# Layer 1's norm of the next image, cut into steps between the attention units

## The chip, the cores and the metric

One core of a Trainium2 chip runs the whole network on a batch of 8 images. The metric is the device time of one execution in microseconds (us), as the median of several runs.

## The reference, cut to what matters

Four residual layers work on x of shape (8, 56, 56, 192). The change concerns layer 1 alone: a group norm over groups of six channels (`_gn`), then a layer norm over the channels inside `_L1_conv_ref`, then shifted-window attention with 7 x 7 windows, 6 heads of 32 channels.

```python
x = x + _L1_conv_ref(_gn(x), ...)      # layer 1

mu = jnp.mean(x, axis=-1, keepdims=True)
var = jnp.var(x, axis=-1, keepdims=True)
x = (x - mu) * jax.lax.rsqrt(var + EPS) * gamma + beta
sx = jnp.roll(x, shift=(-SHIFT[0], -SHIFT[1]), axis=(1, 2))
# windows of 7 x 7, q, k, v by one projection, softmax(q k^T + bias + mask) v, projection, roll back
```

## The kernel before, in words

The layers run one after the other, each image by image, all in float32. Layer 1 lies between about 3000 and 4750 us of the profile.

An image of layer 1 is a tile `x1` of 128 partitions: two half images of 64 channels by three channel chunks j. `rolled` (L489) loads it from DRAM with the shift applied, in 18 DMAs whose rows hold 53 or 3 floats; the same function stores the result in another 18. All 36 are issued on SP's queue. The pool gives `x1` two buffers, so the load of image b+1 needs the buffer of image b-1, which comes free when the store of image b-1 has landed.

`layer1_norm` (L499) makes the normed image `xr`:

- statistics: 12 `bn_stats` on VectorE (L170), aggregates (L171), 14 small matmuls `gh_m` and 14 `gh_v` that sum over channel groups (L181), a square root on ScalarE (L192);
- for each g of four groups of 392 positions: three ScalarE operations that scale and reorder into windows (L516), matmuls for the mean (L523, tile `mean`), a subtraction on VectorE (L525), a square on ScalarE (L527), matmuls for the variance (L529, tile `vps`);
- one square root over all groups (L533), one reciprocal (L534), and for each g a matmul that spreads the result (L538, tile `rstd`) and a multiplication (L540).

The attention of an image is four units, g = 0 to 3, one for each row of windows in both halves. `layer1_scores(g)` (L543) projects q and k (L556), v (L576), forms the scores `S` (L596) and their softmax on VectorE, POOL and ScalarE (L603 to L611). `layer1_mix(g)` (L614) transposes the weights (L626, tile `et_ps`), multiplies with v (L639, `po`), projects (L658, `pr`) and adds into `x1` (L663). The scores of a unit are issued ahead of the mix of the unit before it: scores(u+1), mix(u). The norm of image b+1 is issued as a whole at g = 1 of image b, ahead of scores(b,2) and mix(b,1); the store of image b follows mix(b,3).

The order on each engine is made by the tile framework at build time. It works through the program with costs of its own and lets an instruction pass an earlier one that isn't ready. PSUM tiles come from two tags. Tag "mm" has three buffers: `gh_m`, `gh_v`, `mean`, `rstd`, `qk_ps`, `v_ps`, `po` and `pr` take turns in it. Tag "et" has two: `et_ps`, and before the change `vps`. On the chip every engine, and SP's queue, then works strictly in the order that was made.

Of the kernel before, what the change touches and what calls it, by code (L numbers as in the profile page):

```python
# [10 lines left out]
F32 = mybir.dt.float32  # L11
AF = mybir.ActivationFunctionType
# [8 lines left out]
TT = 392  # L21
# [55 lines left out]
def kernel(ctx: ExitStack, tc: tile.TileContext, a: dict, out: bass.AP):  # L77
    nc = tc.nc
    nimg = a["x"].shape[0]
# [28 lines left out]
    eps5 = const.tile([128, 1], F32, name="eps5")  # L108
# [22 lines left out]
    x2 = [dram.tile([C, NT], F32, name=f"x2_{b}") for b in range(nimg)]  # L131
# [30 lines left out]
    def gn_stats_halves(x, pool, psum, sc, sh, ptag="qv"):  # L162

        n = x.shape[2]
        nt = -(-n // 512)
        st = pool.tile([128, 3, nt, 6], F32, name="gh_st")
        mv = pool.tile([128, 3, 2], F32, name="gh_mv")
        for j in range(3):
            for t in range(nt):
                nc.vector.bn_stats(st[:, j, t, :], x[:, j, bass.ts(t, n // nt)])  # L170
            nc.vector.bn_aggr(mv[:, j, :], st[:, j].rearrange("p t s -> p (t s)"))  # L171

        def over_groups(v, name):
            if ptag == "mm":
                ps = psum.tile([128, 512], F32, name=name, tag="mm", bufs=3)[:, 0:3]
            else:
                ps = psum.tile([128, 2, 512], F32, name=name, tag=ptag)[:, 0, 0:3]
            for j in range(3):
                ks = [k for k in range(3) if abs(j - k) < 2]
                for k in ks:  # L180
                    nc.tensor.matmul(ps[:, j:j + 1], gmath[:, k, j, :], v[:, k:k + 1], start=(k == ks[0]), stop=(k == ks[-1]))  # L181
            return ps


        mean = pool.tile([128, 3], F32, name="gh_mean")
        nc.vector.tensor_scalar(mean, over_groups(mv[:, :, 0], "gh_m"), n / NH, None, ALU.mult)
        d = pool.tile([128, 3], F32, name="gh_d")
        nc.vector.tensor_tensor(d, mv[:, :, 0], mean, ALU.subtract)
        nc.vector.tensor_tensor(d, d, d, ALU.mult)
        nc.vector.tensor_tensor(d, d, mv[:, :, 1], ALU.add)  # L190
        if n == NH:
            nc.scalar.activation(sc, over_groups(d, "gh_v"), AF.Sqrt, bias=eps5)  # L192
        else:

            z = pool.tile([128, 3], F32, name="gh_z")
            nc.vector.scalar_tensor_tensor(z, mean, 1.0 - n / NH, mean, ALU.mult, ALU.mult)
            nc.vector.scalar_tensor_tensor(z, over_groups(d, "gh_v"), n / NH, z, ALU.mult, ALU.add)
            nc.scalar.activation(sc, z, AF.Sqrt, bias=eps5)
        nc.vector.reciprocal(sc, sc)
        nc.vector.scalar_tensor_tensor(sh, mean, -1.0, sc, ALU.mult, ALU.mult)  # L200
# [288 lines left out]
    def rolled(dram_image, tile_image, store):  # L489

        d = dram_image.rearrange("(j p) (h w) -> p j h w", p=64, w=W)
        for s, h0, h1, r0 in ((0, 0, 28, 3), (1, 0, 25, 31), (1, 25, 28, 0)):
            for w0, w1, c0 in ((0, 53, 3), (53, 56, 0)):
                for j in range(3):
                    sb = tile_image[64 * s:64 * s + 64, j, h0:h1, w0:w1]
                    dr = d[:, j, r0:r0 + h1 - h0, c0:c0 + w1 - w0]
                    nc.sync.dma_start(dr, sb) if store else nc.sync.dma_start(sb, dr)  # L497

    def layer1_norm(b, pool, psum, consts):  # L499

        ones2, ones32, sel = consts[4:]
        x = pool.tile([128, 3, H // 2, W], F32, name="x1")
        rolled(x1[b], x, False)
        sc = pool.tile([128, 3], F32, name="sc1")
        sh = pool.tile([128, 3], F32, name="sh1")
        gn_stats_halves(x.rearrange("p j h w -> p j (h w)"), pool, psum, sc, sh, "mm")

        xr = pool.tile([128, 3 * NH + 16], F32, name="xr")
        nc.gpsimd.memset(xr[:, 3 * NH:], 0.0)
        xw = xr[:, 0:3 * NH].rearrange("p (j n) -> p j n", j=3)  # L510

        vps = psum.tile([128, 512], F32, name="vps", tag="et", bufs=2)
        for g in range(4):
            gs = bass.ts(g, TT)
            for j in range(3):
                nc.scalar.activation(  # L516
                    xw[:, j, gs].rearrange("p (w i j) -> p w i j", i=7, j=7),
                    x[:, j, 7 * g:7 * g + 7].rearrange("p i (w j) -> p w i j", j=7), AF.Identity,
                    bias=sh[:, j:j + 1], scale=sc[:, j:j + 1],
                )  # L520
            mp = psum.tile([128, 512], F32, name="mean", tag="mm", bufs=3)[:, 0:TT]
            for j in range(3):
                nc.tensor.matmul(mp, ones2, xw[:, j, gs], start=(j == 0), stop=(j == 2))  # L523
            xs = xw[:, :, gs]
            nc.vector.tensor_tensor(xs, xs, mp.unsqueeze(1).to_broadcast([128, 3, TT]), ALU.subtract)  # L525
            sq = pool.tile([128, 3, TT], F32, name="sq")
            nc.scalar.activation(sq, xs, AF.Square)  # L527
            for j in range(3):
                nc.tensor.matmul(  # L529
                    vps[32 * g:32 * g + 32, 0:TT], ones32, sq[:, j], start=(j == 0), stop=(j == 2)  # L530
                )
        rs = pool.tile([128, TT], F32, name="rs1")
        nc.scalar.activation(rs, vps[:, 0:TT], AF.Sqrt, bias=eps5)  # L533
        nc.vector.reciprocal(rs, rs)  # L534
        for g in range(4):
            gs = bass.ts(g, TT)
            bp = psum.tile([128, 512], F32, name="rstd", tag="mm", bufs=3)[:, 0:TT]
            nc.tensor.matmul(bp, sel[32 * g:32 * g + 32], rs[32 * g:32 * g + 32], start=True, stop=True)  # L538
            xs = xw[:, :, gs]
            nc.vector.tensor_tensor(xs, xs, bp.unsqueeze(1).to_broadcast([128, 3, TT]), ALU.mult)  # L540
        return x, xr

    def layer1_scores(g, xr, pool, psum, S, es, consts):  # L543

# [409 lines left out]
    with ExitStack() as st:  # L954
        pool = st.enter_context(tc.tile_pool(name="qv", bufs=2))
        psum = st.enter_context(tc.tile_pool(name="qvp", bufs=4, space=PSUM))
# [4 lines left out]
        x = layer0_load(0, pool)  # L961
# [7 lines left out]
        for b in range(nimg):  # L969

            between = {i: blocks.pop(0) for i in (1, 7, 12) if blocks}
            ahead = []
            if b + 1 < nimg:
                x = layer0_load(b + 1, pool)
# [5 lines left out]
    with ExitStack() as st:  # L980
        pool = st.enter_context(tc.tile_pool(name="mix", bufs=2))
        psum = st.enter_context(tc.tile_pool(name="mixp", bufs=2, space=PSUM))
# [10 lines left out]
    with ExitStack() as st:  # L993
        pool = st.enter_context(tc.tile_pool(name="l1", bufs=2))
        psum = st.enter_context(tc.tile_pool(name="l1p", bufs=1, space=PSUM))
        consts = layer1_weights(pool, psum)

        ones2 = pool.tile([128, 128], F32, name="ones2", bufs=1)
        ones32 = pool.tile([128, 32], F32, name="ones32", bufs=1)
        sel = pool.tile([128, 128], F32, name="sel", bufs=1)  # L1000
        nc.gpsimd.memset(ones2, 0.0)
        nc.gpsimd.memset(ones32, 0.0)
        for s in range(2):
            nc.gpsimd.memset(ones2[64 * s:64 * s + 64, 64 * s:64 * s + 64], 1.0 / C)
            nc.gpsimd.memset(ones32[64 * s:64 * s + 64, 16 * s:16 * s + 16], 1.0 / C)
        nc.gpsimd.dma_start(sel, a["sel"])
        S = psum.tile([128, 24, 64], F32, name="S")
        nc.vector.memset(S, 0.0)
        es = [[pool.tile([128, 24, 64], F32, name=f"e{k}{s}", bufs=1) for s in range(2)] for k in range(2)]
        for e in es[0] + es[1]:  # L1010
            nc.gpsimd.memset(e, 0.0)

        consts = (*consts, ones2, ones32, sel)
        normed = {0: layer1_norm(0, pool, psum, consts)}
        units = [(b, g) for b in range(nimg) for g in range(4)]
        values = {units[0]: layer1_scores(0, normed[0][1], pool, psum, S, es, consts)}
        for u, (b, g) in enumerate(units):
            if g == 1 and b + 1 < nimg:
                normed[b + 1] = layer1_norm(b + 1, pool, psum, consts)
            if u + 1 < len(units):  # L1020
                b1, g1 = units[u + 1]
                values[b1, g1] = layer1_scores(g1, normed[b1][1], pool, psum, S, es, consts)
            layer1_mix(g, normed[b][0], values.pop((b, g)), pool, psum, es, consts)
            if g == 3:
                rolled(x2[b], normed.pop(b)[0], True)


    with ExitStack() as st:
        pool = st.enter_context(tc.tile_pool(name="l2i", bufs=2))
# [135 lines left out]
```

## Time and profile before

| | us |
|---|---|
| median of 3 runs (lowest, highest) | 8218.3 (8207.87, 8222.58) |
| the profiled execution, its own time | 8152.04 |
| its span | 8149.2 |
| TensorE (PE) busy in the span | 6370.0 (78%) |
| VectorE (DVE), ScalarE (ACT), POOL busy | 3182.6, 1734.7, 480.4 |

The timeline gives the moments of each middle image b: when SP issues the first store of image b-1, the first `bn_stats` for image b+1, the first L516 of its norm, the first q/k matmul of unit (b,2), which stands behind that norm, and the next image's first store.

| image b | first store | first L170 | first L516 | qk of (b,2) | next first store |
|---|---|---|---|---|---|
| 1 | 3281.7 | 3339.5 | 3352.2 | 3395.5 | 3499.8 |
| 2 | 3499.8 | 3559.3 | 3571.9 | 3614.7 | 3722.2 |
| 3 | 3722.2 | 3781.7 | 3794.3 | 3836.7 | 3944.7 |
| 4 | 3944.7 | 4003.2 | 4015.8 | 4057.7 | 4163.4 |
| 5 | 4163.4 | 4222.6 | 4235.5 | 4278.3 | 4384.6 |
| 6 | 4384.6 | 4443.8 | 4456.6 | 4499.2 | 4607.4 |

Read along a row: the image's period is last column less first. Image 0 needs no wait, as both buffers of `x1` are free then; its norm of image 1 runs from 3125.0 (end of the last L663 of unit (0,0)) to 3172.3 (qk of unit (0,2)).

### The profile page before, as it was taken

How to read it: one execution, taken by the hardware profiler on the slowest of the kernel's cores; microseconds unless marked ns; L12 is line 12 of the kernel's file. 1: busy time of each engine (PE TensorE's matmuls, PEld its weight loads, DVE VectorE, ACT ScalarE, POOL GpSimd, SP SyncE). 2: the span in 40 equal slices, each digit the busy share in tenths (PEclk: the TensorE clock that was granted, in tenths of full speed). 3: DMA queues.
4: the chain of work that ended last, by engine and by line, in shares of the span. 5: the costliest groups of instructions: out<-in, count | busy, mean ns of one | idle time of the engine just before them, and what ended most of it. 6: DMA issues, size and time to landing. Idle time of an engine off the chain costs nothing.

```text
span 8149.2 us, 126312 instructions
## 1 busy us (share of the span) xinstructions
PE 6370.0 (78%) x56258; PEld 4179.1 (51%) x56258; DVE 3182.6 (39%) x4598; ACT 1734.7 (21%) x2448; POOL 480.4 (6%) x390
## 2 busy tenths in 40 slices
PE   6799787787877868777777858799968646678899
PEld 4567555555655544444444534566634336644444
DVE  6677522221212224333333346555557540033321
ACT  2234211111111112222222200111135310023333
POOL 4200000000000001111111200000000000000000
PEclk8899888888888878777777878899988758889999
DMA  8998967666677540333333255554458667732221
GB/s 200 196 190 165 191 138 160 148 138 139 133 150 168 121 83 25 49 43 49 43 49 49 44 102 183 183 178 169 168 136 190 150 190 169 173 109 72 71 57 27
DMA packets 1042080, 1018.65 MB, mean 125 GB/s; under 512 B 833812, under 2 KB 964796, under 8 KB 1015272
## 3 DMA queue, kind: packets, MB, share of 16 engines
q1 hardware_dynamic: 1018016, 829.64, 44.4%
q10 hardware_dynamic: 11808, 118.60, 6.8%
q0 software_dynamic: 11712, 62.34, 3.0%
q8 instruction: 441, 7.23, 0.4%
q14 instruction: 103, 0.84, 0.0%
HBM read 668.34 MB, written 342.04 MB: 124 GB/s over the span
## 4 chain that ended last, share of the span: by engine, by line
PE 55%; DMA 17%; DVE 12%; SPq 6%; issue 5%; ACT 4%; POOL 2%; DVEq 0%; POOLq 0%; ACTq 0%
PE op L401 6%; PE qv L349 5%; DMA rt<-toep 5%; PE y L438 5%; PE po L938 5%; PE ph L929 4%; PE cps L872 4%; PE pj L418 4%; SPq L497 4%; PE qk_ps L556 3%; PE mx L755 3%; PE cv L735 3%; DVE ln_st L206 2%; PE pr L658 2%; DMA rt<-qvw 2%
## 5 line engine op out<-in xcount | busy, mean ns | idle before, releaser
L401 PE MATMUL op<-rt,lt 120*56 120x56 f32 x9216 | 683.6, 313 | 319.2 <-DMA rt<-toep 217.3
L401 PEld LDWEIGHTS op<-rt,lt 120*56 120x56 f32 x9216 | 659.6, 224 | 403.7 <-issue 386.4
L349 PE MATMUL qv<-w_qv_sb,xn 64*112 64x288 f32 x5376 | 729.0, 425 | 107.2 <-DVE act L355 107.2
L349 PEld LDWEIGHTS qv<-w_qv_sb,xn 64*112 64x112 f32 x5376 | 556.5, 183 | 277.0 <-DVE act L355 133.2
L418 PE MATMUL pj<-xn,w_p_sb 64*128 64x392 f32 (+1 forms) x1920 | 491.0, 540 | 85.8 <-ACT pp L423 46.7
L872 PE MATMUL cps<-zc,wt 113*128 113x224 f32 x1536 | 322.7, 374 | 210.4 <-DMA zc<-ones_d 165.2
L407 DVE COPY o<-op 120x448 f32<-120x448 f32 (+1 forms) x160 | 99.6, 622 | 902.1 <-PE op L401 886.6
L938 PE MATMUL po<-hid,w_sb 128*64 128x392 f32 x2304 | 398.6, 505 | 52.6 <-ACT hid L933 52.6
L929 PE MATMUL ph<-y,w_sb 64*128 64x392 f32 x2304 | 422.2, 499 | 6.5 <-ACT hid L933 6.5
L438 PE MATMUL y<-pp,w_o_sb 128*64 128x392 f32 (+1 forms) x1920 | 420.7, 517 | 3.6 <-DVE pp L432 1.6
L872 PEld LDWEIGHTS cps<-zc,wt 113*128 113x128 f32 x1536 | 307.7, 201 | 225.4 <-issue 214.2
L356 ACT ACTIVATE act<-act 112x576 f32<-112x576 f32 x448 | 301.1, 683 | 509.5 <-DVE act L355 508.9
L355 DVE TENSOR_TENSOR act<-qv,b_qv 112x576 f32<-112x576 f32 x448 | 317.2, 749 | 39.9 <-PE qv L349 39.9
L556 PE MATMUL qk_ps<-xr,wg 64*96 64x392 f32 x1536 | 327.7, 529 | 3.3 <-ACT qk L562 2.3
L418 PEld LDWEIGHTS pj<-xn,w_p_sb 64*128 64x128 f32 (+1 forms) x1920 | 203.4, 185 | 245.4 <-issue 115.7
L735 PE MATMUL cv<-zc,wt 128*128 128x224 f32 x1536 | 301.2, 355 | 29.9 <-DMA zc<-pd 29.9
L929 PEld LDWEIGHTS ph<-y,w_sb 64*128 64x128 f32 x2304 | 232.4, 189 | 171.5 <-issue 25.9
L423 ACT ACTIVATE pp<-pj,vecs_sb 128x784 f32<-128x784 f32 (+1 forms) x160 | 146.8, 918 | 787.7 <-PE pj L418 754.5
L735 PEld LDWEIGHTS cv<-zc,wt 128*128 128x128 f32 x1536 | 290.2, 189 | 46.3 <-issue 39.3
L938 PEld LDWEIGHTS po<-hid,w_sb 128*64 128x64 f32 x2304 | 164.9, 140 | 282.4 <-issue 223.8
L945 DVE TENSOR_TENSOR x<-x,z 128x392 f32<-128x392 f32 x96 | 54.4, 567 | 643.4 <-ACT z L943 643.4
L693 PE MATMUL pin<-w_in_sb,xn 64*128 64x384 f32 x1392 | 257.1, 516 | 57.3 <-POOL xn L684 38.2
(218 smaller groups left out, 8675.2 us busy)
## 6 DMA issues: line engine op xcount, KB each, us to landing
lt<-toep SPq DMA_DIRECT2D x72, 896.0 KB
rt<-toep SPq DMA_DIRECT2D x72, 896.0 KB
qvh<-qv SPq DMA_DIRECT2D x224, 252.0 KB
qvw<-qv SPq DMA_DIRECT2D x448, 126.0 KB
lt<-qvh ACTq DMA_DIRECT2D x72, 784.0 KB
rt<-qvw ACTq DMA_DIRECT2D x72, 784.0 KB
wt<-in_band_dram SPq DMA_DIRECT2D x24, 2048.0 KB
pd<-pt SPq DMA_DIRECT2D x8, 5568.0 KB
```

Source lines behind the costliest of these rows:

```text
L349: nc.tensor.matmul(ps[s][:, which, 0:D1 // 2], xn[64 * s:64 * s + 64, j, bass.ts(i, 2 * W)], w_qv[64 * s:64 * s + 64, j, which, ns], start ...
L355: nc.vector.tensor_tensor(act, ps[s][:, :, 0:D1 // 2], b_qv[:, :, ns], ALU.add)
L356: nc.scalar.activation(act, act, AF.Silu)
L401: nc.tensor.matmul(op[64 * u:64 * u + W, i, :], lt[0:120, :, d], rt[0:120, :, d], start=True, stop=True)
L418: nc.tensor.matmul(ps[0:M, s, 0:TT], w_p[64 * s:64 * s + 64, j, d0:d0 + M], xn[64 * s:64 * s + 64, j, ts], start=(j == 0), stop=(j == 2),)
L438: nc.tensor.matmul(y[64 * s:64 * s + 64], w_o[0:M, c, 64 * j:64 * j + 64], pp[0:M, s], start=(c == gated[0][0]), stop=(c == gated[-1][0]),)
L497: nc.sync.dma_start(dr, sb) if store else nc.sync.dma_start(sb, dr)
L556: nc.tensor.matmul(ps[s], wg[64 * s:64 * s + 64, j, c0:c0 + HC], xw[64 * s:64 * s + 64, j, gs], start=(j == 0), stop=(j == 2),)
L735: nc.tensor.matmul(dst, wt[:, c4 + i, 128 * q:128 * q + 128], zc[:, :, c4 + i, q:q + NPAIR], start=(q == 0), stop=(q == 1),)
L872: nc.tensor.matmul(dst.rearrange("p (b n) -> p b n", n=NPAIR), wt[:, c4 + i, (3 - q) * OP:(4 - q) * OP], zc[:, :, c4 + i, q:q + NPAIR], st ...
L929: nc.tensor.matmul(ps[:, s, 0:TT], w0[64 * s:64 * s + 64, j, m * 128:(m + 1) * 128], y[64 * s:64 * s + 64, j, ts], start=(j == 0), stop=(j ...
L938: nc.tensor.matmul(ps[64 * s:64 * s + 64], w1[:, m, 64 * j:64 * j + 64], hid[:, m, s], start=(m == 0), stop=(m == 5),)
```

## The change

`layer1_norm` becomes a generator that stops (`yield`) after the issue of the load, after the statistics, after each group's square, after each group's square root, after the reciprocal, and after each group's last multiplication. The driving loop takes these steps by a plan of three numbers for each unit: `first` and `second` steps ahead of the scores, `third` steps between scores and mix. The driver's order for a middle image b is, after the store of image b-1:

- g = 0: load(b+1), statistics(b+1), scores(b,1), both parts of group 0, mix(b,0)
- g = 1: both parts of group 1, scores(b,2), both parts of group 2, mix(b,1)
- g = 2: both parts of group 3, reciprocal, scores(b,3), last step of group 0, mix(b,2)
- g = 3: last step of group 1, scores(b+1,0), last steps of groups 2 and 3, mix(b,3), store(b)

The variance tile moves from tag "et" to tag "mm", one for each group in place of one for all, and the square root is taken group by group on 32 partitions. The memset of the padding of `xr` and the tile of `rs` are made ahead of the statistics.

```diff
     def layer1_norm(b, pool, psum, consts):
...
         rolled(x1[b], x, False)
+
+        xr = pool.tile([128, 3 * NH + 16], F32, name="xr")
+        nc.gpsimd.memset(xr[:, 3 * NH:], 0.0)
+        xw = xr[:, 0:3 * NH].rearrange("p (j n) -> p j n", j=3)
+        rs = pool.tile([128, TT], F32, name="rs1")
+        yield x, xr
...
         gn_stats_halves(x.rearrange("p j h w -> p j (h w)"), pool, psum, sc, sh, "mm")
-
-        xr = pool.tile([128, 3 * NH + 16], F32, name="xr")
-        nc.gpsimd.memset(xr[:, 3 * NH:], 0.0)
-        xw = xr[:, 0:3 * NH].rearrange("p (j n) -> p j n", j=3)
-
-        vps = psum.tile([128, 512], F32, name="vps", tag="et", bufs=2)
+        yield
         for g in range(4):
...
             nc.scalar.activation(sq, xs, AF.Square)
+            yield
+            vp = psum.tile([128, 512], F32, name="vps", tag="mm", bufs=3)[32 * g:32 * g + 32, 0:TT]
             for j in range(3):
-                nc.tensor.matmul(
-                    vps[32 * g:32 * g + 32, 0:TT], ones32, sq[:, j], start=(j == 0), stop=(j == 2)
-                )
-        rs = pool.tile([128, TT], F32, name="rs1")
-        nc.scalar.activation(rs, vps[:, 0:TT], AF.Sqrt, bias=eps5)
+                nc.tensor.matmul(vp, ones32, sq[:, j], start=(j == 0), stop=(j == 2))
+            nc.scalar.activation(rs[32 * g:32 * g + 32], vp, AF.Sqrt, bias=eps5[32 * g:32 * g + 32])
+            yield
         nc.vector.reciprocal(rs, rs)
+        yield
         for g in range(4):
...
             nc.vector.tensor_tensor(xs, xs, bp.unsqueeze(1).to_broadcast([128, 3, TT]), ALU.mult)
-        return x, xr
+            yield
...
-        for u, (b, g) in enumerate(units):
-            if g == 1 and b + 1 < nimg:
-                normed[b + 1] = layer1_norm(b + 1, pool, psum, consts)
-            if u + 1 < len(units):
-                b1, g1 = units[u + 1]
-                values[b1, g1] = layer1_scores(g1, normed[b1][1], pool, psum, S, es, consts)
-            layer1_mix(g, normed[b][0], values.pop((b, g)), pool, psum, es, consts)
-            if g == 3:
-                rolled(x2[b], normed.pop(b)[0], True)
+        plan = [(1, 1, 2), (1, 1, 2), (1, 2, 1), (0, 1, 2)]
+        for b in range(nimg):
+            x = images[b][0]
+            steps = layer1_norm(b + 1, pool, psum, consts) if b + 1 < nimg else iter(())
+            for g in range(4):
+                first, second, third = plan[g]
+                for _ in range(first):
+                    ahead = next(steps, None)
+                    if ahead:
+                        images.append(ahead)
+                for _ in range(second):
+                    next(steps, None)
+                following = None
+                if g < 3 or b + 1 < nimg:
+                    xr = images[b][1] if g < 3 else images[b + 1][1]
+                    following = layer1_scores((g + 1) % 4, xr, pool, psum, S, es, consts)
+                for _ in range(third):
+                    next(steps, None)
+                layer1_mix(g, x, values, pool, psum, es, consts)
+                values = following
+            for _ in steps:
+                pass
+            rolled(x2[b], x, True)
```

More of the change, by code (lines that the diff above doesn't have):

```diff
@@ L1013 @@
         consts = (*consts, ones2, ones32, sel)
-        normed = {0: layer1_norm(0, pool, psum, consts)}
-        units = [(b, g) for b in range(nimg) for g in range(4)]
-        values = {units[0]: layer1_scores(0, normed[0][1], pool, psum, S, es, consts)}
-        for u, (b, g) in enumerate(units):
-            if g == 1 and b + 1 < nimg:
-                normed[b + 1] = layer1_norm(b + 1, pool, psum, consts)
-            if u + 1 < len(units):
-                b1, g1 = units[u + 1]
-                values[b1, g1] = layer1_scores(g1, normed[b1][1], pool, psum, S, es, consts)
-            layer1_mix(g, normed[b][0], values.pop((b, g)), pool, psum, es, consts)
-            if g == 3:
-                rolled(x2[b], normed.pop(b)[0], True)
+        steps = layer1_norm(0, pool, psum, consts)
+        images = [next(steps)]
+        for _ in steps:
+            pass
+        values = layer1_scores(0, images[0][1], pool, psum, S, es, consts)
+        plan = [(1, 1, 2), (1, 1, 2), (1, 2, 1), (0, 1, 2)]
[18 more added lines that the diff above has]
+                values = following
+            for _ in steps:
+                pass
+            rolled(x2[b], x, True)
     with ExitStack() as st:
```

## The prediction

> **What bounds the kernel now.** I read the page first (TensorE is busy 78% of the span and leads the chain of work that ended last), then the windows of one image of layer 1, then the timeline of that image, then TensorE's waits. The windows of image 2, cut at the store's start, the norm's first L516, the first qk behind the norm and the next store (columns: window, its length, busy time and count of PE, PEld, DVE, ACT, POOL, then clock, DMA share, GB/s):
>
> ```profile
> 3499.80:3571.90 72.10, 44.48 (x705) 28.39 (x701) 23.29 (x42) 10.66 (x17) 8.71 (x4) 0.68 0.88 85
> 3571.90:3614.70 42.80, 28.82 (x81) 11.43 (x81) 12.59 (x11) 15.73 (x21) 0.00 (x0) 0.78 0.00 1
> 3614.70:3722.20 107.50, 93.77 (x1988) 58.46 (x1989) 43.70 (x55) 28.92 (x46) 26.21 (x13) 0.82 0.11 36
> ```
>
> In the last window, three attention units, PE is busy 93.77 of 107.5 us: the units are bound by PE, with some 4.6 us idle each. The first two windows hold one unit and the norm, and there PE waits. In the timeline (start, length, engine, line, what, in brackets the idle time before it and its releaser):
>
> ```profile
> 3499.80 34.87 SPq L497 DMA_DIRECT2D x<-x  x18
> ...
> 3536.01 26.23 SPq L497 DMA_DIRECT2D x<-x  x18
> ...
> 3546.80 0.63 DVE L663 SCALAR_TENSOR_TENSOR x<-pr,bpr,x 128x392 f32<-128x392 f32 x1 [1.35 <-PE pr L658]
> 3559.28 4.34 DVE L170 BATCH_NORM_STATS2 gh_st<-x 128x6 f32<-128x392 f32 x9 [11.86 <-DMA x<-x]
> ...
> 3563.93 3.22 PE L181 MATMUL gh_m<-gh_mv,gmath_sb 128*128 128x1 f32 x14 [17.17 <-DVE gh_mv L171]
> ...
> 3568.08 3.12 PE L181 MATMUL gh_v<-gh_d,gmath_sb 128*128 128x1 f32 x14 [0.94 <-DVE gh_d L190]
> ...
> 3572.73 4.20 PE L523 MATMUL mean<-xr,ones 128*128 128x392 f32 x6 [1.54 <-ACT xr L516]
> ...
> 3579.62 3.67 PE L529 MATMUL vps<-sq,ones 128*32 128x392 f32 x6 [2.69 <-ACT sq L527]
> ...
> 3590.89 2.14 PE L523 MATMUL mean<-xr,ones 128*128 128x392 f32 x6
> ...
> 3609.91 1.68 PE L538 MATMUL rstd<-rs,sel 32*128 32x392 f32 x6 [3.31 <-DVE rs L534]
> ...
> 3614.65 3.69 PE L556 MATMUL qk_ps<-xr,wg 64*96 64x392 f32 x8
> ```
>
> Two things are to be seen. First, x of image b+1 can't arrive before some 60 us after the end of image b-1: 18 stores (34.87 us) and, on the same queue and into the buffer that they free, 18 loads (26.23 us). Unit (b,0) covers 47 us of that; then everything waits. Second, no qk matmul passes the norm. Its inputs were there long before, and PE stood idle for 17.17, 2.69 and 3.31 us while `gh_m`, `vps` and `rstd` weren't ready, with all three "mm" buffers free at the first and the third. Only the transposes L626, whose tag is "et", slip in, and even they come after the first `vps`, which stands ahead of them in that tag. In all of layer 1 the first matmuls into the tiles of one tag stand in the order of the code. I take it as the rule of this plan: **buffers of one tag are handed out in program order, so an "mm" tile whose data is late holds back every later "mm" tile.**
>
> TensorE's waits from 3395 to 4607 us, which hold five norms (waiter, releaser, total, times, longest):
>
> ```profile
> PE gh_m L181 <- DVE gh_mv L171: 101.9, 5, 22.8
> PE po L639 <- issue: 40.3, 20, 3.7
> PE vps L529 <- ACT sq L527: 27.2, 10, 2.8
> PE rstd L538 <- DVE rs L534: 16.6, 5, 3.3
> ```
>
> **What the Trainium skill says.** "DMA: Bandwidth & Descriptors", Specifications: full rate needs at least 512 bytes in a piece. The rows here are 212 and 12 bytes, and while they move the DMA engines are taken 0.88 of the time at 85 GB/s: agrees. "TensorE: Matmul & The Clock Gate", What's actually happening: after an idle window PE runs at half rate until it has been busy for some 3.4 us. The first six `mean` matmuls after the wait take 4.20 us, later ones 2.14: agrees. "ScalarE: Activation LUTs", Table sets: exp followed by sqrt needs a table load each way. The trace has 16 loads in layer 1, two for each image, at 1.283 us.
>
> **The change part by part**, for a middle image, counted from the first store (S).
>
> 1. *Load and statistics ahead of scores(b,1).* SP's order stays: the load stood right behind the store already, so nothing is gained there; the bias loads that follow it aren't needed until S(b,1). POOL's memset of 0.11 us waits for nothing late. But `gh_m` and `gh_v` are now ahead of `qk_ps` of scores(b,1) in "mm". PE waits for x; queued behind the wait are all of scores(b,1) and the `po` and `pr` of mix(b,0), and through them DVE's, ACT's and POOL's work on them. Before, that unit ran during store and load. From 3499.80 to the end of `gh_v` (3571.2) it is **71.4 us**; the other images agree within 1.5.
> 2. *Cold clock* for the first qk: `mean` showed 2.1 us lost. **+2.5**, between 0 and 4.
> 3. *Unit (b,0)* now runs behind the wait, free of the store's traffic. Plain units (qk to qk: 3428.7 to 3501.7, 3649.6 to 3725.1, 3871.6 to 3947.3, two each) take 36.5, 37.75 and 37.85: **37.4**. The 48 transposes of mix(b,0), tag "et", can run during the wait: 24 of them were 4.3 us of PE's time in the old norm; **-5**, between 0 and -7.
> 4. *The other three units*: qk of (b,2) to the next store is 104.3, 107.5, 108.0, 105.7, 106.3, 108.2 in the six images, mean **106.7**; the 24 transposes of mix(b,1) no longer ride in a norm: **+2**.
> 5. *The norm's matmuls between the units*, N. Warm, four `mean` groups at 2.14, four `vps` at 2.16 and `rstd` at 1.7 make 18.9 us of PE. Part lands where PE idles: the wait ahead of `po` is up to 3.7 us, and `mean`/`vps` of groups 0 and 2 stand just ahead of `po`: -6, between 0 and -10. But in groups 1 and 3 `vps` follows `mean` with only transposes between, as qk is behind both: the subtraction (1.38) and the square (1.18) are open, 2.8 us as in the trace, twice: +5.6, between 0 and +10. Four square roots on ACT in place of one (0.587 each; on 32 partitions I take the same) and the table goes back and forth up to eight more times (1.283 each) ahead of copies that free "mm" buffers: some 12 us of ACT, which has 72% free; +3 on PE, between 0 and +6. VectorE's work is unchanged and hidden by PE. **N = 21.5**, between 9 and 35.
>
> Sum: 71.4 + 2.5 + 37.4 - 5 + 106.7 + 2 + 21.5 = 236.5 us. Before, the six periods from 3281.7 to 4607.4 average 220.95. **+15.5 us for each of six images, +93.** What was saved (47 - 21.5 of the norm's own time) is less than the cover that unit (b,0) gave.
>
> 6. *Image 0* has its second x early (landed by about 3040), so no wait: its norm took 47.3 us alone; now 6 for the statistics' matmuls, 2 for transposes and N: **-17.8**. Norm 0 and image 7 are as before.
>
> Total +75 us. Against the profiled execution's own 8152.04 that is 8227; the median of runs, 8218.3, lies 66 us above that execution, and I add the same 75 to it: **8293 us**.
>
> **The rivals.**
> - *A: the order isn't binding* (other side: faster). If scores(b,1) pass the waiting `gh_m`, x lands behind their cover and nothing waits: four units of 37.4, 4 for the first unit under the store's traffic (41.6 on average), 2, N and 6 for `gh`: 183 us, -38 for each of six images and -18: 7973. It decides if the first qk of (b,1) starts before x has landed, S+60. For it: PE's idle time is that large. Against: the tag order, kept without exception through long idle times.
> - *B: a wash.* The wait is as forecast, but the norm's matmuls nearly all fall into idle PE time: N about 10 to 14 puts the total (7N - 75) within 16 us: 8218. For it: 4.6 idle us in each unit. Against: half of that is short drains ahead of transposes and `pr`, where no norm matmul stands.
> - *C: the steps hurt the units*, through table loads and `vps` waits, N = 35: +170, 8388. For it: ScalarE's copies free the buffers of every qk and v. Against: ACT is busy 29 of 107 us.
>
> **How the numbers follow.** Forecast with C as its upper part 0.79, B 0.09, A 0.12. 0.2% (16 us) is about what a measurement of this kernel can tell from no change. The ends: N = 12 gives +9, N = 35 with the worst of points 2 to 4 about +180. Range 8224 to 8398, which leaves out A and half of B. Slower 0.79, same 0.09, faster 0.12, by the same cases.
>
> **What would show it.** Right: in each of images 1 to 6 PE idles some 60 us from the store's start, ended by `gh_m`; the first qk of (b,1) stands behind `gh_v` at S+71; L516 starts at S+72 as before; afterwards no wait for x; periods near 236. Point 5: `mean` and `vps` at 2.1 us a group, ten table loads an image at most, units at 37 plus some 5. Wrong: a qk of (b,1) ahead of `gh_m`, or L170 not waiting for the DMA (A); periods near 221 with full units (B).

## The result and the profile after

The changed kernel takes 8266.7 us (median of 4 runs, 8263.26 to 8273.41), the kernel before 8213.08 (4 runs, 8205.24 to 8222.58): ratio 1.0066, 95% interval 1.0048 to 1.0083. It is slower by 54 us, as forecast in sign; forecast were 75 (8293).

The profiled execution of the changed kernel has a span of 8262.3 us. The first one of the kernel before (8149.2) lay under all its other runs, so a second was taken: span 8200.1, own time 8201.9, which still is 11 us under the median. Unless said otherwise, "before" below is that second trace.

First the windows of image 2 in the changed kernel, cut at the first store, the end of `gh_v` and the next first store (columns as in the prediction):

```profile
3507.70:3583.40 75.70, 12.42 (x63) 9.39 (x59) 9.65 (x23) 3.04 (x4) 0.00 (x0) 0.55 0.97 64
3583.40:3750.60 167.20, 145.82 (x2713) 83.06 (x2715) 70.70 (x83) 60.74 (x89) 34.95 (x17) 0.85 0.10 31
```

and the same cut in the kernel before, second trace:

```profile
3510.20:3585.30 75.10, 45.17 (x705) 29.31 (x701) 23.04 (x40) 10.51 (x16) 9.20 (x5) 0.64 0.91 82
3585.30:3735.30 150.00, 121.14 (x2067) 70.01 (x2069) 56.44 (x66) 44.91 (x68) 26.24 (x13) 0.81 0.08 26
```

Store, load and statistics last 75 us in both. Before, PE is busy 45 us in that stretch, since unit (b,0) runs in it; now 12. The second stretch is 17 us longer: it has taken over the 37 us of a unit and given back some 20. It is also denser: PE is busy 87% of it, before 81%.

The timeline of image 2 in the changed kernel (line numbers of the changed code):

```profile
3507.66 66.60 SPq L497 DMA_DIRECT2D x<-x  x36
...
3513.70 0.66 PE L629 MATMUL et_ps<-ident,e 128*128 128x128 f32 x4 [0.28 <-ACT et L634]
...
3571.12 4.73 DVE L170 BATCH_NORM_STATS2 gh_st<-x 128x6 f32<-128x392 f32 x9 [56.91 <-DMA x<-x]
...
3576.07 3.30 PE L181 MATMUL gh_m<-gh_mv,gmath_sb 128*128 128x1 f32 x14 [61.72 <-DVE gh_mv L171]
3580.22 3.15 PE L181 MATMUL gh_v<-gh_d,gmath_sb 128*128 128x1 f32 x14 [0.84 <-DVE gh_d L190]
3583.29 11.51 PE L559 MATMUL qk_ps<-xr,wg 64*96 64x392 f32 x48
...
3600.92 2.24 PE L525 MATMUL mean<-xr,ones 128*128 128x392 f32 x6
...
3608.58 3.76 PE L533 MATMUL vps<-sq,ones 128*32 128x392 f32 x6 [3.89 <-ACT sq L529]
...
3619.65 2.24 PE L525 MATMUL mean<-xr,ones 128*128 128x392 f32 x6
...
3624.64 2.16 PE L533 MATMUL vps<-sq,ones 128*32 128x392 f32 x6
...
3675.72 9.49 PE L559 MATMUL qk_ps<-xr,wg 64*96 64x392 f32 x48
```

One wait of 61.72 us ends at `gh_m`, and the q and k of scores(b,1) stand right behind `gh_v`. After that nothing waits for x. TensorE's waits in the six middle images, changed kernel, then before ("issue" is idle time in which PE waited for nothing that the profile shows):

```profile
PE gh_m L181 <- DVE gh_mv L171: 360.7, 6, 61.7
PE vps L533 <- ACT sq L529: 44.2, 12, 4.6
...
PE po L642 <- issue: 11.6, 7, 3.4
PE S L599 <- issue: 11.1, 15, 1.5
```

```profile
PE gh_m L181 <- DVE gh_mv L171: 133.2, 6, 27.0
PE po L639 <- issue: 43.8, 22, 4.9
PE vps L529 <- ACT sq L527: 32.6, 12, 2.8
PE S L596 <- issue: 29.4, 24, 4.0
...
PE rstd L538 <- DVE rs L534: 19.9, 6, 3.3
```

The wait at `gh_m` grew by 228 us, while the norm's other waits taken together and the idle times put down to "issue" shrank; only the wait of `vps` for the square grew. PE's busy time shrank too, for nearly the same number of matmuls (the six images of the changed kernel, then before):

```profile
3267.99:4704.19 1436.20, 930.42 (x16634) 551.13 (x16632) 481.48 (x636) 382.77 (x558) 209.49 (x101) 0.77 0.37 42
3286.62:4642.91 1356.29, 994.33 (x16632) 588.60 (x16630) 476.78 (x636) 332.92 (x504) 209.41 (x101) 0.77 0.36 44
```

So an image has 24.0 us more of idle time and 10.7 us less of busy time. From the first store of image 0 to that of image 6, the mean period is 239.4 us in the changed kernel and 226.05 before (220.95 in the first trace).

### The profile page after: what moved, and what is told of

Read it like the earlier page. It is cut to its first block, busy times and chain, and to the rows that moved or that the text cites. A ratio compares the mean times of both kernels' runs of the same rounds, so it can differ in the third digit from the quotient of the medians.

```text
span 8262.3 us, 126345 instructions
## 1 busy us (share of the span) xinstructions
PE 6329.3 (77%) x56258; PEld 4158.1 (50%) x56258; DVE 3190.1 (39%) x4598; ACT 1797.8 (22%) x2516; POOL 479.7 (6%) x390
## 4 chain that ended last, share of the span: by engine, by line
PE 53%; DMA 17%; DVE 11%; SPq 7%; issue 5%; ACT 4%; POOL 2%; DVEq 0%; POOLq 0%; ACTq 0%
PE op L401 5%; DMA rt<-toep 5%; PE qv L349 5%; PE po L941 4%; PE y L438 4%; SPq L497 4%; PE ph L932 4%; PE cps L875 4%; PE pj L418 4%; PE qk_ps L559 4%; PE mx L758 3%; PE cv L738 3%; PE pr L661 2%; DVE ln_st L206 2%; DMA x<-x 2%
## 5 line engine op out<-in xcount | busy, mean ns | idle before, releaser
L181 PE MATMUL gh_m<-gh_mv,gmath_sb 128*128 128x1 f32 x336 | 56.1, 291 | 461.7 <-DVE gh_mv L171 461.0
L170 DVE BATCH_NORM_STATS2 gh_st<-x 128x6 f32<-128x392 f32 (+1 forms) x288 | 144.3, 557 | 440.9 <-DMA x<-x 421.8
```

## The experiments

Each kernel was run beside the kernel before on the same chip. "Period" is the mean of the same six images, from first store to first store.

**x3: a third buffer for x1.** If the wait comes from `gh_m` standing ahead of scores(b,1) while x is late, making x early must end it, with the order of the steps unchanged.

```diff
-        wg = pool.tile([128, 3, 3 * C], F32, name="wg", bufs=1)
+        wg = w_qkv
...
-        x = pool.tile([128, 3, H // 2, W], F32, name="x1")
+        x = pool.tile([128, 3, H // 2, W], F32, name="x1", bufs=3)
...
-            sq = pool.tile([128, 3, TT], F32, name="sq")
+            sq = pool.tile([128, 3, TT], F32, name="sq", bufs=1)
...
-            o = pool.tile([HC, 2, TT], F32, name=f"oa{s}")
+            o = pool.tile([HC, 2, TT], F32, name=f"oa{s}", bufs=1)
```

> The changed kernel with three buffers for the tile x1 in place of two, so that the load of image b+1 doesn't need the store of image b-1; to make room, the product tile wg takes the place of w_qkv, and sq and oa have one buffer each. The computation is the same. Theory (tag order: the statistics' matmuls stand ahead of scores(b,1) and wait for x): the wait at gh_m in images 1 to 6 falls from 60 us to below 10, the period from 239 to about 185 us, the time to about 7935 us. Rival 1 (the steps between the units are what costs, through table loads and waits for the variance tile): the wait goes, but units stretch, and the time stays above 8200. Rival 2 (the transfers are the limit wherever they stand): x is still late, the time near 8200.

Measured: 7909.73 us, ratio to before 0.9638 (0.9623 to 0.9653), period 180.3. The wait is gone. In the timeline of x3 `gh_m` follows `pr` with no idle time, and image b+1 was loaded and its `bn_stats` done during image b-1:

```profile
3334.30 1.44 DVE L170 BATCH_NORM_STATS2 gh_st<-x 128x6 f32<-128x392 f32 x3
...
3440.99 11.19 SPq L497 DMA_DIRECT2D x<-x  x5
3443.65 1.72 PE L181 MATMUL gh_m<-gh_mv,gmath_sb 128*128 128x1 f32 x14
...
3447.20 1.63 PE L181 MATMUL gh_v<-gh_d,gmath_sb 128*128 128x1 f32 x14
...
3448.76 2.87 PE L559 MATMUL qk_ps<-xr,w_qkv_sb 64*96 64x392 f32 x14
```

The DMA engines move the same bytes, so neither the transfers (rival 2) nor the steps (rival 1) held the changed kernel back. This version beats both kernels.

**late_stats: the same steps, another plan.**

```diff
-        plan = [(1, 1, 2), (1, 1, 2), (1, 2, 1), (0, 1, 2)]
+        plan = [(1, 0, 0), (0, 0, 1), (2, 2, 2), (2, 3, 2)]
```

> The changed kernel with another plan of steps alone: load at g=0, statistics between scores(b,2) and mix(b,1), groups 0 to 2 in unit 2, the rest in unit 3. Theory (tag order): unit (b,0) and scores(b,2) run under store and load again, the wait at gh_m falls to under 15 us, the period to about 205 us though the groups are now crowded, the time to about 8060 us. Rival 1 (the steps cost): no gain or a loss against 8267, since the steps are denser. Rival 2 (the transfers are the limit): no wait is saved, 8267.

Measured: 7979.53 us, ratio 0.9715 (0.9699 to 0.9731), period 189.8. With the two buffers of x1 and nothing but the place of the steps changed, the waits at `gh_m` fall to 3.6 to 10.7 us in the six images. The crowded groups cost less than I gave them (period 190, not 205), and the time is 80 us under the expectation.

**whole_early: the norm unsplit, at the changed kernel's place.** It takes the change apart from the other side: the earlier place alone.

```diff
-            if g == 1 and b + 1 < nimg:
+            if g == 0 and b + 1 < nimg:
```

> The kernel before with one edit: the whole norm of image b+1 is issued at g=0 of image b, ahead of scores(b,1), in place of g=1; nothing is split. Theory (tag order): the wait of 60 us at gh_m appears as in the changed kernel and the unsplit norm of 43 us comes on top: period about 257 us, about 8430 us. The difference to the changed kernel, some 18 us an image, is what the splitting alone brings. Rival 1 (the steps are what costs): this kernel has no steps and is no slower than the kernel before by more than the wait of an image, faster than the changed kernel.

Measured: 8411.08 us, ratio 1.0244 (1.0229 to 1.0259), period 259.7; waits at `gh_m` of 61.9 to 64.1 us. The earlier place costs 259.7 - 226.05 = 33.7 us an image, and splitting (with the variance tile's move to "mm", which comes with it) gives back 259.7 - 239.4 = 20.3. So the change is a loss and a gain, and the loss is larger. Rival 1 fails: without steps the kernel is 144 us slower than the changed one.

**before_again: a second trace of the kernel before**, with no edit.

> The kernel before once more, for a second trace of it, as its first profiled execution (8152 us) lay under its other runs. Expected: layer 1 as long as in the first trace (1751 us from the first load to the last L663), periods of 221 us, and the missing 60 us in other layers.

Measured: 8201.9 us, period 226.05. The expectation missed: layer 1, from the first load to the last L663, isn't as long as in the first trace but 27 us longer (1778 against 1751 us). From the first store to the end of `gh_v` the images take 74.1 to 76.1 us here and 69.8 to 71.4 there. About half of what the first execution had been quicker by lay in layer 1, in the stretch that waits for these transfers.

**gh_et: order or lateness.** x stays late, but the two statistics tiles leave the tag.

```diff
             if ptag == "mm":
-                ps = psum.tile([128, 512], F32, name=name, tag="mm", bufs=3)[:, 0:3]
+                ps = psum.tile([128, 512], F32, name=name, tag="et", bufs=2)[:, 0:3]
```

> The changed kernel with one edit: the PSUM tiles gh_m and gh_v of layer 1 are taken from tag et in place of tag mm; the order of the steps is the same. Theory (tag order): qk, v and S of scores(b,1), whose tags are mm and S, now run during the wait for x, and only mean of group 0 and the transposes of mix(b,0) stay behind it. PE does some 20 us of work in the wait and loses the 3 us of transposes: period 239 to about 223 us, time about 8170 us. Rival (x is late and order has no part in it, the wait belongs to the load alone): the wait stays as it is, 8267 us.

Measured: 8140.79 us, ratio 0.992 (0.9906 to 0.9935), period 218.55. In the timeline of gh_et, qk, v and S of scores(b,1) now run ahead of the late `gh_m`, and its wait is 38 us in place of 62:

```profile
3493.46 9.48 PE L559 MATMUL qk_ps<-xr,wg 64*96 64x392 f32 x48
3502.88 2.69 PE L579 MATMUL v_ps<-wg,xr 64*64 64x96 f32 x106
...
3518.80 1.83 PE L599 MATMUL S<-qk 32*49 32x49 f32 x96 [1.50 <-DVE e L606]
3558.47 3.31 PE L181 MATMUL gh_m<-gh_mv,gmath_sb 128*128 128x1 f32 x14 [37.84 <-DVE gh_mv L171]
```

Data, order of steps and late x are the same; only the tag of two tiles differs. So the order within the tag is what held q, k, v and S behind the wait, and the rival falls. In the 38 us that are left PE runs nothing: the transposes of mix(b,0) now stand behind `gh_m` and `gh_v` in "et", and its `po` needs these and stands behind `mean` of group 0 in "mm". This run doesn't tell the two apart.

**before_x3: the third buffer without the steps.** The four edits of x3, in the kernel before.

> The kernel before (norm whole, at g=1) with three buffers for x1 and the same room made for them (wg in w_qkv's place, one buffer for sq and oa). Theory: x is there when the norm begins, so the wait of some 22 us at gh_m and the part of the statistics that VectorE can do earlier go: period 226 to about 200 us, about 8055 us. What the steps then bring beside it (x3 was 7910 us, period 180.8) is about 20 us an image: the norm's own chain of waits. Rival (the third buffer alone is the gain, the steps bring nothing or cost): 7910 us or less.

Measured: 8054.83 us, ratio 0.9821 (0.9805 to 0.9838), period 201.8. The buffer alone brings 226.05 - 201.8 = 24 us an image; the steps bring another 201.8 - 180.3 = 21.5 on top, about what whole_early showed (20.3). The expectation put this down to the norm's chain of waits. That is the smaller part. The windows of the six images, before_x3, then x3 (columns as in the prediction):

```profile
3286.23:4497.09 1210.86, 984.97 (x16636) 580.47 (x16634) 469.16 (x621) 333.34 (x504) 209.25 (x101) 0.79 0.40 48
3261.53:4343.51 1081.98, 908.31 (x16636) 539.72 (x16633) 473.37 (x621) 394.57 (x570) 209.58 (x101) 0.86 0.44 53
```

The same 16636 matmuls keep PE busy 12.8 us less for each image, at a granted clock of 0.86 in place of 0.79; its idle time falls by 8.7 us. Why the matmuls get faster is not isolated; that PE stands idle in fewer places fits the clock reading of the prediction. In the idle time, the waits at `rstd` go, but those for the square hardly change (before_x3, before_x3, x3):

```profile
PE rstd L538 <- DVE rs L534: 19.9, 6, 3.3
...
PE vps L529 <- ACT sq L527: 32.6, 12, 2.8
...
PE vps L533 <- ACT sq L529: 28.3, 12, 3.7
```

**no_groups: N by itself.**

```diff
                     bias=sh[:, j:j + 1], scale=sc[:, j:j + 1],
                 )
-            mp = psum.tile([128, 512], F32, name="mean", tag="mm", bufs=3)[:, 0:TT]
...
             yield
-            vp = psum.tile([128, 512], F32, name="vps", tag="mm", bufs=3)[32 * g:32 * g + 32, 0:TT]
...
             yield
-        nc.vector.reciprocal(rs, rs)
         yield
         for g in range(4):
-            gs = bass.ts(g, TT)
...
             yield
```

> The changed kernel without mean, subtraction, square, variance, square root, reciprocal and last multiplication of layer 1's layer norm (all left out, for all images; the scaling into windows stays). It measures N, the cost of the norm's group steps between the units, forecast at 21.5 us an image and 22.3 by the sum of the changed kernel's trace. Theory: the wait of 60 us at gh_m stays as it is, the period falls from 239 to about 217 us, and with the exposed group part of the first image's norm (40 us) the time is about 8070 us. Rival (table loads and waits in the units cost more than this, N near 35): about 7980 us.

Measured: 8103.01 us, ratio 0.9876 (0.9861 to 0.9891), period 218.7. N = 239.4 - 218.7 = 20.7 us, forecast 21.5. The waits of 59.4 to 61.7 us at `gh_m` stay. The whole saving is 33 us under the expectation: image 0 gained 10 us, not N, and image 7, which has no norm, took 8 us more than in the changed kernel (PE busy 2.7 us more and idle 5.0 us more, at a granted clock of 0.83 in place of 0.86). Why it did isn't settled.

**x3_onesqrt: fewer table loads.**

```diff
-            nc.scalar.activation(rs[32 * g:32 * g + 32], vp, AF.Sqrt, bias=eps5[32 * g:32 * g + 32])
+            nc.vector.tensor_copy(rs[32 * g:32 * g + 32], vp)
             yield
+        nc.scalar.activation(rs, rs, AF.Sqrt, bias=eps5)
         nc.vector.reciprocal(rs, rs)
```

> x3 with one more edit: the variances of the four groups are copied to SBUF by VectorE, and one square root over all of them is taken ahead of the reciprocal, as in the kernel before; so the activation table changes for it once an image, not four times. Theory (N is PE work and the wait for the square; table loads are hidden by the 70% of ScalarE's time that is free): table loads fall from 72 to about 30, and the time by 0 to 20 us from 7910. Rival (table loads are a main part of N): 50 us or more come off.

Measured: 7915.76 us, ratio 0.9646 (0.9632 to 0.9661), beside 0.9638 (0.9623 to 0.9653) for x3. 42 table loads fewer (30, not 72) make no difference that can be told. In the six images the period is 179.0 us beside 180.3 for x3, in one trace each, which is less than two traces of one kernel differ (220.95 and 226.05). As far as can be told they are hidden.

## Why the prediction was right

- **The rule.** "Buffers of one tag are handed out in program order" was read off the order of one trace, and it carried the sign. gh_et tests it directly, by the tag alone; x3 and late_stats show that the wait goes when x is early or is asked for late. Rival A would have had a qk of (b,1) ahead of `gh_m`; none is in the changed kernel.
- **Point 1, the wait: 71.4 us forecast, 73.7 measured** (72.6 to 75.7), the mean from first store to the end of `gh_v`. The transfers took longer than in the trace that I had. There the six images agree within 1.7 us, not 1.5 (69.8 to 71.4), and 71.4 was the longest.
- **Point 2, cold clock: +2.5 forecast, +2.0 measured.** In image 2 the first 48 qk matmuls take 11.51 us, later ones 9.49.
- **Points 2 to 5, the rest of the period: 165.1 forecast, 165.7 measured** (239.4 - 73.7). That this is so close is in part luck, as errors cancel. Inside it I misread one count: a unit has 24 transposes in six tiles, not 48; the trace shows 20 of them in the wait, worth 2.8 us rather than 5. The 24 in the old norm were a whole unit's, so the +2 was too small by about as much.
- **N: 21.5 forecast, 20.7 by no_groups.** Here too the parts were less good than the sum. The norm's matmuls take 23.3 us of PE's time an image in the changed kernel, not 18.9, since some are slow after a wait (`vps` of group 0 takes 3.76 us, where 2.16 was counted). PE's other matmuls take 3.6 us less than in no_groups; the sum had no term for that. Idle time is 1.0 us more. Compared with the kernel before, idle time at `po` and S put down to "issue" fell from 73.2 to 22.7 us over six images, 8.4 an image, where I gave 6. The open waits for the square came in the wrong groups: 1 and 3 are covered by transposes, while 0 and 2 wait 3.89 and 3.21 us in image 2, as VectorE and ScalarE have the softmax ahead of them there. Total 44.2 us, 7.4 an image; I had 5.6. The +3 for table loads was too much: layer 1 has 60 of them in the changed kernel and 16 before, but x3_onesqrt shows next to nothing to save.
- **Point 6, image 0: -17.8 forecast, -16.0 measured** (first qk of the image to the first store: 196.9 us, before 212.9).
- **The total: +75 forecast, +54 measured.** Between the trace of the changed kernel and the second one before, the periods and image 0 give 6 x (239.4 - 226.05) - 16.0 = +64, as their spans do (62). The first trace was quick in the period before (220.95), but also in the wait that I took from it, so most of this cancels: with wait, units and period all read from the second trace (75.2, 37.1, 107.2 and 226.05) the same sum gives 6 x (240.5 - 226.05) - 17.8 = +69. So treating the 66 us by which that trace lay low as an offset outside the sum did little harm. The 10 us between +64 and +54 stay open; the interval of the measured difference, 39 to 68, holds +64 too. In the range, the lower end should have been 8227 by the +9 that stands beside it, not 8224.

Rival B (a wash) fails by the interval, whose lower end is 1.0048. Rival C fails by no_groups and x3_onesqrt.

## What to carry to other kernels

A step that is cut up and moved earlier takes its buffers with it: look up which tag each of its tiles is in and what comes after in that tag, since a tile whose data is late holds back everything behind it, however ready. Ask first when the data can be there (here about 60 us after the end of image b-1, by store and load), and place the first consumer behind that, or make the data earlier; the same steps were 54 us slower, 229 us faster (late_stats) or, with one more buffer, 299 us faster than before. And read the old time and the new terms of a small forecast from one and the same execution: the sum came to +75 with one trace and +69 with the other, but taking the period alone from the second would have given +45.

## What the runs showed of the hardware

- The same 18 stores and 18 loads don't always take the same time: first store to the end of `gh_v` 69.8 to 71.4 us in one execution of the kernel before, 74.1 to 76.1 in another. The difference lies in the stretch of the stores: the first load is issued 35.7 to 36.7 us after the first store in the one, 39.7 to 42.6 in the other.
- The order of the work is fixed before it runs. In the two traces of the kernel before, PE, VectorE, ScalarE and POOL go through layer 1 in the same order (22224 matmuls on PE), although x came some 4 us later in the second.
- PE's small matmuls take longer beside the store's traffic. In x3, v and S of unit (b,1) take 14.4 to 20.4 us from the first v to the last S in images 1 to 6, with transfers under way; in the changed kernel, with the same order of steps and the DMA engines busy some 0.1 of the time, 9.6 to 10.9 us. Of that, idle time put down to "issue" is 2.1 to 5.5 us in x3 and at most 1.2 in the changed kernel. That the transfers cause the rest is likely, but no run here isolates it.
- PE's idle times put down to "issue" look, for the most part, like waits for instructions. The page of the changed kernel has this DMA queue (packets, MB, share of the 16 engines' time):

```profile
q8 instruction: 441, 7.23, 0.4%
```

  That is one packet of 16384 bytes for about every 256 matmuls and weight loads of PE in the whole program. In the six images of the changed kernel and of the second trace before, PE has 40 such idle times of over 1 us, and 37 of them end 1.0 to 2.7 us after a packet of this queue has ended; of moments picked at random some 16% do. While the transfers of x run, such a packet takes longer: 1.55 us in the median, 3.3 at most, beside 0.98 without them (second trace before). This is inferred from the times, as no run changes how instructions are fetched. It would explain why these idle times shrink where the norm's long matmuls stand between short ones: 256 instructions then last longer.
